# Text rows first in the stacks, first entry's copies on GpSimd, and the second pair's keys begun ahead of slot 0

## The chip, the cores and the metric

The kernel runs on one core of a Trainium2 chip. The metric is the device time of one execution in microseconds. The engines are TensorE (PE, with PEld for its weight loads), VectorE (DVE), ScalarE (ACT), GpSimd (POOL) and SyncE (SP, which here only issues DMAs). In the profile a time stands from the start of the span; `L747` is line 747 of the kernel before. The PE clock is given as a share of full speed.

## The reference, cut to what matters

Two cross-attention layers follow each other over 16 batch entries of 256 rows, with 20 heads of 16. The 256 context rows are split into text and image rows: 77 and 179 in the first layer, 252 and 4 in the second. The first layer, which the change touches, computes

```python
q_h, k_h, v_h = heads(x @ Wq), heads(text @ Wk), heads(text @ Wv)
text_out = softmax(q_h k_h * scale) v_h
text_probs = softmax((q . k_text) * scale)          # over all channels, one for all heads
sem = (text_probs @ text) . ip * scale
fused = q_h ip_k_h * scale + 0.5 * sem               # ip = image rows, their own Wk_ip, Wv_ip
out = (text_out + softmax(fused) * mask @ ip_v_h) @ Wout + bout + x
```

and the second has the same parts with normalized semantic scores. All data is fp32. A product is made from a high part (rounded to fp32r) and a low part (what the rounding left), in three matmuls: high by high, high by low, low by high.

## The kernel before

The first layer has 80 slots: slot k is entry b = k // 5 and group g = k % 5 of four heads. The second layer has 80 more. In a slot, `score0(k + 2, t)` (L747) makes plain scores from which VectorE takes row maxima (L748, L749); `maxima0` (L755 to L759) turns the maxima, copies them to tile `mt` and sends them by four small DMAs into the query stack; `turned0(k, t)` (L771) makes the transposed scores less the maxima, ScalarE takes the exponential (L774), GpSimd multiplies by the semantic factor `rs` (L777); `attend0(k - 1)` (L806) multiplies with the values and VectorE and GpSimd settle the result (L817 to L824, into `hsn`).

Scores come from two stacks in rings of four, `qs[k % 4]` and `ks[k % 4]`, 127 rows each: 48 field rows (high, low, high parts of 16 channels), 77 text rows that carry the semantic part, and 2 rows for the maxima (in `ks`: two indicator rows). `stacks0(k, parts)` fills them: "K" and "Q" fetch field rows from DRAM (`kd`, `qd`), "T" fetches the text rows of the query stack from `tph`, "M" those of the key stack from `M`. Text rows are the same for all groups of an entry, so they are fetched only for g < 4. In the kernel before, all four parts are DMAs on SP's queue, and the `tph` and `M` tiles have three extra rows so that one DMA fills rows 48 to 127. `fields()` writes the indicator rows and those extra rows.

Keys are made for pairs of entries. `keys0(c)` loads the context of pair c in four tiles (`context`, `in_turn`: a load, a ScalarE cast for the high part, a subtraction for the low part) and then makes keys in six products, text (`wk0`, tile `wA`) and image (`wki0`, tile `wB`) for each of three row blocks. `queries0(b)` loads an input, splits it (`split`, L284 to L286: cast, subtraction of two tiles, and the low part of rows 64 to 127 of the third tile), and projects it (`project`, L611 and L614). `weights4(0)` loads the output weights (`wF`), which entry 0 needs first in slot 7.

What sets the order: `begin()` is everything ahead of slot 0, and there all engines run in the order in which the code is written. Generators are cut into steps; `parts(x)` makes one step of task x, and what a task has left is made in the slots at the times in its list (`FIRST`, `shifted`; -1 means before slot 0). In the slots only TensorE keeps the written order; that of the others is settled when the program is built. SP's DMAs signal eight semaphores in turn, so each issue waits until the DMA eight before it has landed.

## Time and profile before

| | |
|---|---|
| timed runs | 1486.59 us, median of 3 (1484.38 to 1487.22) |
| profiled execution | 1494.71 us, with a span of 1492.9 us |
| granted PE clock, mean | 0.986 |
| busy share of the span | PE 95%, DVE 79%, ACT 59%, POOL 81% |
| first layer's slots | from the first L771 at 50.6 us on |
| moved by DMA | 234.32 MB, 157 GB/s on average; 220 GB/s in the first 100 us |

A row of the timeline has start, length, engine, line, operation, out<-in, shape and count, and in brackets the idle time before it with what ended it. A row of the windows has the stretch, its length, busy time of each engine with its count of instructions, the granted clock, the mean busy share of the DMA engines and GB/s.

### The profile page before, as it was taken

To read this page: it belongs to the slowest core of one execution; us is meant where nothing else is said; L and a number is where in the kernel's file an instruction comes from. 1 tells how busy PE (TensorE), PEld (TensorE's weight loads), DVE (VectorE), ACT (ScalarE), POOL (GpSimd) and SP (SyncE) were. 2 spreads that over 40 slices of the span, in tenths; PEclk is the share of its full clock that TensorE was granted. 3 is DMA by queue.
4 is the path that set the end of the run, shared out by engine and by line. 5 is a ranking of instruction groups with operands and counts; after the bars stand their busy time and mean duration, and the time that the engine had idled before them with its cause. 6 is when DMAs were issued, how large, how long until landed. Compare 5 with 4: busy or idle time off the path is not lost.

```text
span 1492.9 us, 36116 instructions
## 1 busy us (share of the span) xinstructions
PE 1425.3 (95%) x12740; PEld 1153.4 (77%) x12740; DVE 1176.8 (79%) x2595; ACT 885.7 (59%) x1975; POOL 1213.8 (81%) x1302
## 2 busy tenths in 40 slices
PE   7799999999999999789999999999999999999998
PEld 7677888888888787567777777777777777777766
DVE  5578777777777776878887888888878887888787
ACT  6355565656565555456665666666656665666563
POOL 4369797979797877788698789878987888788887
PEclk9899999999999998999999999999999999999999
DMA  7967777777777775775544444434444444443311
GB/s 235 235 180 200 207 222 206 217 205 222 202 226 204 209 200 148 194 208 151 166 99 132 117 123 120 132 115 125 121 126 121 124 118 124 123 126 102 111 32 54
DMA packets 230986, 234.32 MB, mean 157 GB/s; under 512 B 39127, under 2 KB 200678, under 8 KB 230790
## 3 DMA queue, kind: packets, MB, share of 16 engines
q1 hardware_dynamic: 228598, 230.71, 55.6%
q8 instruction: 102, 1.67, 0.5%
q10 hardware_dynamic: 2208, 1.30, 0.4%
q14 instruction: 78, 0.64, 0.1%
HBM read 118.04 MB, written 77.04 MB: 131 GB/s over the span
## 4 chain that ended last, share of the span: by engine, by line
PE 74%; DVE 8%; DMA 6%; POOL 4%; issue 4%; ACT 3%; SPq 1%; ACTq 0%; DVEq 0%; POOLq 0%
PE X L945 15%; PE X L241 14%; PE P L806 6%; PE X L611 5%; PE P L957 5%; PE S L747 5%; PE P L967 4%; PE T L771 4%; PE T L896 3%; PE S L902 3%; PE X L614 2%; PE X L251 2%; PE X L580 2%; DVE mn L749 1%; POOL P L777 1%
## 5 line engine op out<-in xcount | busy, mean ns | idle before, releaser
L777 POOL TENSOR_TENSOR P<-P,rs 128x512 f32<-128x512 f32 x320 | 414.9, 1319 | 85.1 <-ACT P L774 84.0
L936 POOL TENSOR_TENSOR wt<-P,ctb 128x512 f32<-128x512 f32 x318 | 408.4, 1308 | 74.8 <-ACT ctb L934 74.7
L945 PE MATMUL X<-ctb,gm 128*128 128x512 f32 x1120 | 306.3, 402 | 5.8 <-DVE wt L946 5.7
L774 ACT ACTIVATE P<-T 128x512 f32<-128x512 f32 x320 | 175.5, 594 | 155.7 <-PE T L771 106.7
L946 DVE TENSOR_TENSOR wt<-X,wt 128x512 f32<-128x512 f32 x320 | 216.0, 681 | 42.3 <-PE X L945 37.6
L945 PEld LDWEIGHTS X<-ctb,gm 128*128 128x128 f32 x1120 | 195.0, 188 | 39.3 <-DVE wt L946 8.7
L916 ACT ACTIVATE P<-T 128x512 f32<-128x512 f32 x320 | 173.0, 593 | 75.2 <-PE T L896 72.2
L934 ACT ACTIVATE ctb<-P 128x512 fp32r<-128x512 f32 x320 | 186.5, 627 | 36.8 <-PE X L945 34.2
L904 DVE TENSOR_REDUCE mn<-S 128x4 fp32r<-128x1008 f32 x160 | 191.4, 1197 | 0.0
L749 DVE TENSOR_REDUCE mn<-S 128x4 fp32r<-128x716 f32 x160 | 142.3, 889 | 0.0
L806 PE MATMUL P<-P,vr 128*32 128x256 f32 x1920 | 127.4, 397 | 5.4 <-DVE tmp L823 1.9
L747 PE MATMUL S<-ks,qs 125*128 125x256 f32 x640 | 115.7, 304 | 3.9 <-DVE mn L749 1.9
L747 PEld LDWEIGHTS S<-ks,qs 125*128 125x128 f32 x640 | 87.5, 192 | 38.7 <-issue 20.7
L1036 POOL TENSOR_TENSOR r<-u,rs 128x40 f32<-128x40 f32 (+2 forms) x17 | 108.7, 6394 | 3.0 <-DVE u L1033 2.9
L771 PE MATMUL T<-qs,ks 127*128 127x256 f32 x640 | 107.6, 290 | 1.2 <-DMA qs<-mt 0.9
L817 DVE STREAM_TRANSPOSE nt<-P 128x512 f32<-128x512 f32 x80 | 56.9, 712 | 53.2 <-PE P L806 52.7
L806 PEld LDWEIGHTS P<-P,vr 128*32 128x32 f32 x1920 | 56.9, 112 | 47.6 <-issue 7.6
L771 PEld LDWEIGHTS T<-qs,ks 127*128 127x128 f32 x640 | 90.9, 195 | 3.3 <-DMA qs<-mt 0.7
L748 DVE TENSOR_REDUCE mn<-S 128x4 fp32r<-128x308 f32 x160 | 74.4, 465 | 22.2 <-PE S L747 22.0
L957 PE MATMUL P<-P,v1t 128*32 128x256 f32 x1280 | 85.7, 385 | 0.0
L967 PE MATMUL P<-wt,zone 128*32 128x256 f32 x1280 | 84.4, 379 | 0.0
L241 PE MATMUL X<-wC,cta 128*128 128x324 f32 (+1 forms) x474 | 78.6, 312 | 0.0
(305 smaller groups left out, 2979.9 us busy)
## 6 DMA issues: line engine op xcount, KB each, us to landing
qd<-q SPq DMA_DIRECT2D x96, 256.0 KB
qs<-tph SPq DMA_DIRECT2D x64, 320.0 KB
rawc<-in_cT_dram SPq DMA_DIRECT2D x60, 256.0 KB
qs<-qd SPq DMA_DIRECT2D x80, 192.0 KB
ks<-kd SPq DMA_DIRECT2D x80, 192.0 KB
ks<-kd SPq DMA_DIRECT2D x160, 96.0 KB
qs<-qd SPq DMA_DIRECT2D x160, 96.0 KB
kd<-kst SPq DMA_DIRECT2D x57, 256.0 KB
```

The source lines that it names most:

```text
L241: last = mm(out, lhs(a, k), rhs(b, k), start=i == 0, stop=i == len(terms) - 1)
L747: mm(sp[:, h], Q[: XROW + T0, h, t * 128 : (t + 1) * 128], K[: XROW + T0, h], start=True, stop=True)
L771: mm(st[p][:, j], K[:KS0, 2 * p + j, t * 128 : (t + 1) * 128], Q[:KS0, 2 * p + j], start=True, stop=True)
L774: exp = anchor(nc.scalar.activation(pt, st[p], AF.Exp, scale=SCALE))
L777: anchor(nc.gpsimd.tensor_mul(pt, pt, rs[:, t : t + 1].to_broadcast([128, 2, S])))
L806: mm(pv[32 * s : 32 * s + 32, o : o + S], v[:, vt, h : h + 32], P[k, s // 2][:, t, s % 2], start=vt < 2, stop=vt != 1,)
L904: anchor(nc.vector.tensor_reduce(maxes[k + 2][:, t], sp[:, :, :T1], axis=AX.X, op=ALU.max))
L916: anchor(nc.scalar.activation(P[k, u][:, t], st[u], AF.Exp, scale=SCALE))
L934: nc.scalar.activation(R[k, u][:, t], P[k, u][:, t], AF.Copy, scale=0.5)
L936: anchor(eng.tensor_sub(W[k, u][:, t], P[k, u][:, t], f(R[k, u][:, t])))
L945: mm(yp, gm[:, gb], R[k, u][:, kt], start=i == 0, stop=i == len(blocks[n]) - 1)
L946: nc.vector.tensor_mul(W[k, u][:, n], yp, W[k, u][:, n])
```

## The change

The stacks are laid out anew: text rows first (0 to 76), then 48 field rows (`FIELD` = 125 is their end), then the two rows of maxima. `tph` and `M` lose their three extra rows, and `fields()` writes four wide indicator DMAs and nothing else. For entry 0 the text rows of all four stacks are copied by GpSimd, for the other entries still by DMA. In `begin()` the loads, casts and subtractions of the second pair's context are made among the steps of the second entry (one subtraction on VectorE, three on GpSimd), and its first key product is cut into four pieces, which stand in slot 0. The third entry's input is loaded and split in `begin()` too. In each `queries0` after the first, the third tile's low part is a GpSimd subtraction of 64 rows in place of a VectorE operation on 128. `mt` has two buffers. The output weights are loaded in slots 4 to 5 in place of 2.6 to 3.2, and the context of entry 2 in the second layer is subtracted by GpSimd.

```diff
-TR = T0 + 3
+FIELD = T0 + 48
...
-        yield from in_turn(parts, wait, "rawc raw" if b == 2 and n == 2 else "rawc", nc.gpsimd if wait and b != 2 else nc.vector, n == 2 and b >= 2)
+        yield from in_turn(parts, wait, "rawc raw" if b == 2 and n == 2 else "rawc", nc.vector if not wait else nc.gpsimd if n == 1 or b != 2 else (nc.vector,) + (nc.gpsimd,) * 3, n == 2 and b >= 2)
...
-        order(nc.vector.scalar_tensor_tensor(hl[:, 2], f(hl[:, 2]), neg, src[:, 2], op0=ALU.mult, op1=ALU.add))
+        if neg is None:
+            order(eng.tensor_sub(hl[64:, 2], src[64:, 2], f(hl[64:, 2])))
+        else:
+            order(nc.vector.scalar_tensor_tensor(hl[:, 2], f(hl[:, 2]), neg, src[:, 2], op0=ALU.mult, op1=ALU.add))
...
         for i in range(SIZES["NR"]):
-            dma(ks[i][XROW + T0 : KS0, :, :T0], ind0r[:2, :T0].unsqueeze(1).to_broadcast([2, 4, T0]))
-        for i in range(2):
-            dma(buf("M", [TR, 2, S], FR, bufs=SIZES["M"])[T0:, 0], ind0r)
-            dma(buf("tph", [TR, 2, S], FR, bufs=2)[T0:, 0], ind0r)
+            dma(ks[i][FIELD:KS0], ind0r.unsqueeze(1).to_broadcast([2, 4, S]))
...
-                prod_m(kp, w, m, lambda s, k: ct(s, k)[:, :, lo:hi], 4)
+                if c == 1 and not m + a:
+                    for k in range(4):
+                        for i, (x, y) in enumerate(((0, 0), (0, 1), (1, 0))):
+                            mm(kp, w(x, k, m), ct(y, k)[:, :, lo:hi], start=k + i == 0, stop=k + i == 5)
+                        if k < 3:
+                            yield
+                else:
+                    prod_m(kp, w, m, lambda s, k: ct(s, k)[:, :, lo:hi], 4)
...
-        xs = split(x, tmask[:, 5:6], nc.gpsimd, "hq") if b else xs0.pop()
+        xs = split(x, None, nc.gpsimd, "hq") if b else xs0.pop()
...
             if part == "K":
-                anchor(dma(K[0:XROW], stack_rows(kd[0][b // 2][:, :, b % 2], g)))
+                anchor(dma(K[T0:FIELD], stack_rows(kd[0][b // 2][:, :, b % 2], g)))
...
+                copy = dma if b else lambda out, in_: nc.gpsimd.tensor_copy(out, f(in_))
                 if part == "T":
-                    dma(Q[XROW : XROW + TR], tph[:, 0:1].to_broadcast([TR, 4, S]))
+                    copy(Q[:T0], tph[:, 0:1].to_broadcast([T0, 4, S]))
...
-        mt = buf("mt", [8, S], FR)
+        mt = buf("mt", [8, S], FR, bufs=2)
...
-    FIRST = {"k0": [-1, 0.6, 0.6, 0.6, 1, 1.2, 1.6, 1.6, 2, 2.2, 2.6], "s0": [-1, -1, -1, -1, -1, 0.2, 0.6]}
+    FIRST = {"k0": [-1, -1, -1, -1, -1, 0.2, 0.2, 0.6, 0.6, 1.2, 1.6, 2, 2.2, 2.6], "s0": [-1, -1, -1, -1, -1, 0.2, 0.6]}
...
-    task(("w4", 0), [2.6, 2.8, 3, 3.2], lambda: weights4(0), ("k0", 1))
+    task(("w4", 0), [4, 4.2, 4.6, 5], lambda: weights4(0), ("k0", 1))
...
+        for k in range(SIZES["NR"]):
+            stacks0(k, "M")
...
-        stacks0(0, "TQK")
+        for k in range(SIZES["NR"]):
+            stacks0(k, "T")
+        stacks0(1, "Q")
+        stacks0(2, "Q")
         get(*s0)
         parts(q1, q1)
-        stacks0(1, "M")
+        for k in range(3):
+            stacks0(k, "K")
         parts(v0)
-        stacks0(1, "TQK")
         parts(v0)
         get(*v0)
+        parts(q2)
+        parts(k1)
+        stacks0(3, "QK")
```

Three places show how instructions move. The first is TensorE around slot 0, where the second pair's first key product stands (`wA` holds the text key weights, `cta` and `ctb` the pair's context). Before:

```order
L747 MATMUL S<-ks_101,qs_97 128x256 x4
L771 MATMUL T<-qs_95,ks_99 128x256 x4
L747 MATMUL S<-ks_101,qs_97 128x256 x4
L771 MATMUL T<-qs_95,ks_99 128x256 x4
L755 MATMUL X<-ident_r,mn_576 8x128 x2
L747 MATMUL S<-ks_102,qs_98 128x256 x4
L771 MATMUL T<-qs_96,ks_100 128x256 x4
L241 MATMUL X<-cta_81,wA_85 128x156 x3
L241 MATMUL X<-cta_82,wA_85 128x156 x3
L241 MATMUL X<-ctb_83,wA_85 128x156 x3
L241 MATMUL X<-ctb_84,wA_85 128x156 x3
```

And of the change (its L755, L779 and L763 are L747, L771 and L755 of before):

```order
L755 MATMUL S<-ks_101,qs_97 128x256 x4
L779 MATMUL T<-qs_95,ks_99 128x256 x4
L383 MATMUL X<-cta_81,wA_85 128x156 x3
L383 MATMUL X<-cta_82,wA_85 128x156 x3
L755 MATMUL S<-ks_101,qs_97 128x256 x4
L779 MATMUL T<-qs_95,ks_99 128x256 x4
L383 MATMUL X<-ctb_83,wA_85 128x156 x3
L383 MATMUL X<-ctb_84,wA_85 128x156 x3
L763 MATMUL X<-ident_r,mn_585 8x128 x2
L755 MATMUL S<-ks_102,qs_98 128x256 x4
L779 MATMUL T<-qs_96,ks_100 128x256 x4
L241 MATMUL X<-cta_81,wB 128x360 x3
```

The twelve key matmuls move from behind slot 1's first turned scores to two places among slot 0's, and the image key product (`wB`) comes ahead of the first attend. From the third input's projection on, TensorE's order is the same in both.

The second place is GpSimd from the values' low parts (`wD`) to slot 0's multiplication (`P` with `rs`). Before:

```order
L1273 TENSOR_TENSOR wD<-rs_115,wD 128x320
L436 MEMSET M_260 77x2x77
L1273 TENSOR_TENSOR wD<-xc_116,wD 128x320 x2
L436 MEMSET M_261 77x2x77
L777 TENSOR_TENSOR P_120<-P_120,rs_114 128x512
L777 TENSOR_TENSOR P_121<-P_121,rs_114 128x512
```

And of the change:

```order
L1282 TENSOR_TENSOR wD<-xc_116,wD 128x320 x2
L724 CAST qs_95<-tph_439 77x1024
L724 CAST qs_96<-tph_439 77x1024
L724 CAST qs_97<-tph_439 77x1024
L724 CAST qs_98<-tph_439 77x1024
L285 TENSOR_TENSOR hq_230<-xq_91,hq_230 128x512
L287 TENSOR_TENSOR hq_230<-xq_91,hq_230 64x256
L169 TENSOR_TENSOR cta_82<-rawc_118,cta_82 128x512
L169 TENSOR_TENSOR ctb_83<-raw,ctb_83 128x512
L444 MEMSET M_282 77x2x77
L169 TENSOR_TENSOR ctb_84<-raw,ctb_84 128x512
L785 TENSOR_TENSOR P_120<-P_120,rs_114 128x512
```

Four copies into the query stacks, the third entry's split and three context subtractions now stand between the two; four copies into the key stacks (`CAST ks<-M`, 77 by 4 by 179) stand earlier, ahead of the second entry's split.

The third place is SP's queue up to the maxima of slot 0 (`qs_95<-mt`). Before:

```order
L86 DMA qs_97<-tph_263 80x4x256
L86 DMA ks_101<-M_260 80x4x179
L86 DMA ks_102<-kd_70 48x4x256
L86 DMA qs_98<-qd_309 48x1024
L759 DMA qs_95<-mt_222 2x256 x4
L86 DMA qs_98<-tph_263 80x4x256
L86 DMA ks_102<-M_260 80x4x179
L86 DMA rawc_117<-in_cT_dram 128x512
L86 DMA rawc_118<-in_cT_dram 128x512
L86 DMA raw<-in_cT_dram 128x512 x2
L759 DMA qs_96<-mt_222 2x256 x4
L86 DMA qd_495<-q_145 128x2x256 x3
```

And of the change:

```order
L86 DMA xq_91<-in_xT_dram 128x3x256
L86 DMA rawc_117<-in_cT_dram 128x512
L86 DMA rawc_118<-in_cT_dram 128x512
L86 DMA raw<-in_cT_dram 128x512 x2
L86 DMA qs_98<-qd_303 48x1024
L86 DMA ks_102<-kd_70 48x4x256
L86 DMA kd_70<-kst_158 128x2x256
L86 DMA kd_70<-kst_158 128x256
L86 DMA qd_498<-q_144 128x2x256 x3
L86 DMA qd_498<-q_144 64x2x256
L86 DMA qd_498<-q_144 64x256
L767 DMA qs_95<-mt_222 2x256 x4
```

The four context loads (`rawc`, `raw`), the second entry's queries to DRAM and part of its keys now stand ahead of slot 0's maxima; slot 1's maxima follow directly behind.

More of the change, by code (lines that the diff above doesn't have):

```diff
@@ L200, in in_turn @@
             if i:
-                halves(*ahead.pop(0), eng, wait)
+                halves(*ahead.pop(0), eng[i - 1] if isinstance(eng, tuple) else eng, wait)
             for j in new:
@@ L210, in in_turn, with weights @@
                 yield
-    def weights(w_d, tag, half=None, wait=0, raw="raw"):
+    def weights(w_d, tag, half=None, wait=0, raw="raw", later=False):
         n = w_d.shape[1]
@@ L217, in weights @@
         heads = tag != "wF"
-        yield from in_turn([(rows(w_d, k)[:, : n if heads else CH], *rounded(w[:, k], heads)) for k in range(kt)], wait, raw)
+        yield from in_turn([(rows(w_d, k)[:, : n if heads else CH], *rounded(w[:, k], heads)) for k in range(kt)], wait, raw, later=later)
         if half is not None:
@@ L443, in tokens0 @@
         yield
[L444 removed]
+        return M
     v1t, gmt = [], []
@@ L518, in weights4 @@
     def weights4(l):
-        wo.append((yield from weights((wo0_d, wo1_d)[l], "wF", tmask[:, 4:5], (0.1, 0.3)[l], "rawc")))
+        wo.append((yield from weights((wo0_d, wo1_d)[l], "wF", tmask[:, 4:5], (0.1, 0.3)[l], "rawc", not l)))
     def weights3():
@@ L1362, in begin @@
         parts(v1)
+        parts(k1)
         get(*v1)
         parts(s1)
+        parts(k1, k1)
         score0(1, 1)
@@ L1367, in begin @@
         maxima0(1, nc.sync)
-        for make in held:
-            make()
-        parts(k0)
+        parts(k1)
+        parts(k0, k0)
         resid0.append(load(xT_d[0], "xc"))
```

51 lines of the change are left out of this document (25 added, 26 removed).

## The prediction

> **What bounds the kernel now.** I read the windows of busy time first, to see in which stretches TensorE is short of work, then its timeline there, then the timelines of the engine that each of its waits names.
>
> ```profile
> span 1492.9 us, 36116 instructions
> ...
> core 0: us, PE busy (x) PEld busy (x) DVE busy (x) ACT busy (x) POOL busy (x), PEclk, DMA share, GB/s
> 0.00:57.00 57.00, 44.80 (x288) 41.66 (x288) 32.68 (x94) 32.91 (x84) 22.87 (x45) 1.00 0.84 230
> 57.00:71.60 14.60, 10.66 (x68) 8.19 (x66) 9.05 (x14) 3.71 (x8) 8.07 (x8) 0.65 0.85 240
> 71.60:83.42 11.82, 10.47 (x90) 9.35 (x90) 7.68 (x16) 6.32 (x16) 7.37 (x10) 1.00 0.77 216
> 83.42:102.74 19.32, 17.64 (x145) 13.99 (x146) 12.38 (x32) 8.49 (x22) 11.49 (x12) 0.91 0.61 167
> ...
> 320.00:380.00 60.00, 59.64 (x568) 51.56 (x566) 45.29 (x110) 36.19 (x87) 53.55 (x53) 1.00 0.79 220
> ```
>
> In a steady stretch of the first layer (320 to 380) TensorE is busy 59.64 of 60 us: there the end is set by TensorE's own work, which this change leaves as it is, matmul for matmul. In the first 102.74 us it is busy 83.57, and from 57 to 71.6 its granted clock is 0.65. A change to the order at the start can win only there, and a microsecond won there goes through to the end, since TensorE is the bound behind it and its order from the third input's projection on is unchanged. Where the time lies, in TensorE's timeline, with the idle time before a row and its releaser in brackets:
>
> ```profile
> 50.63 0.92 PE L771 MATMUL T<-qs,ks 127*128 127x256 f32 x4
> 52.17 0.74 PE L747 MATMUL S<-ks,qs 125*128 125x256 f32 x4 [0.63 <-DVE mn L749]
> 54.29 0.23 PE L755 MATMUL X<-ident_r,mn 128*8 128x128 f32 x1 [0.84 <-DVE mn L749]
> 55.64 0.93 PE L771 MATMUL T<-qs,ks 127*128 127x256 f32 x4 [0.42 <-DMA qs<-mt]
> 59.49 0.72 PE L241 MATMUL X<-cta,wA 128*128 128x156 f32 x2 [2.31 <-DVE cta L169]
> 61.16 1.35 PE L241 MATMUL X<-ctb,wA 128*128 128x156 f32 x5 [0.75 <-DVE ctb L169]
> 62.45 2.79 PE L806 MATMUL P<-P,vr 128*32 128x256 f32 x24
> ...
> 69.09 0.79 PE L241 MATMUL X<-cta,wA 128*128 128x156 f32 x6
> ...
> 71.60 1.10 PE L611 MATMUL X<-hq,wE 128*128 128x256 f32 x7 [0.89 <-POOL hq L285]
> ...
> 76.57 1.50 PE L806 MATMUL P<-P,vr 128*32 128x256 f32 x24
> ...
> 83.42 0.76 PE L241 MATMUL X<-cta 128*77 128x192 f32 x6 [1.35 <-DVE q L169]
> ...
> 92.98 0.23 PE L755 MATMUL X<-ident_r,mn 128*8 128x128 f32 x1 [1.19 <-DVE mn L749]
> ```
>
> The sum is made against the profiled execution, 1494.71 us, which is 1.8 us more than its span and 8.1 us over the runs' median of 1486.59. I carry the difference over to the median unchanged.
>
> **The change part by part.** The second pair's context is the late thing between 56 and 62 us. Its loads stand behind slot 0's maxima on SP's queue, and its subtractions on VectorE between the maxima reductions:
>
> ```profile
> 24.67 3.31 SPq L86 DMA_DIRECT2D qd<-q  x5
> ...
> 44.88 2.62 SPq L759 DMA_DIRECT2D qs<-mt  x4
> ...
> 50.14 1.33 SPq L86 DMA_DIRECT2D rawc<-in_cT_dram  x2
> ...
> 57.66 1.78 DVE L169 TENSOR_TENSOR cta<-rawc,cta 128x512 fp32r<-128x512 f32 x1
> ```
>
> In the change the loads stand directly behind the three key stacks and one input, with 14 DMAs less ahead of them (8 of text rows, 4 of indicator rows into `M` and `tph`, a second load of the indicator, and `hop`). With about 0.65 us an issue (2.62 for 4) they go out from 37 to 40 us, and land by 45. ScalarE casts the tiles among the second entry's steps, the last behind slot 1's maxima at about 49.5. GpSimd's three subtractions (1.3 us each, as L777's below) end at about 51.3 us. TensorE asks for the first two tiles after slot 0's first turned scores, at about 51.1, and for the others after one key half, scores and turned scores (some 1.8 us) at 52.9.
>
> *Up to slot 0's turned scores I count nothing.* TensorE waits 1.33 and 0.45 us for stacks before 45 us, and both should shrink; but the turned scores at 50.63 need the maxima's DMAs, and these now stand behind more bytes.
>
> ```profile
> 34.00:38.00 4.00, 4.00 (x30) 4.00 (x29) 0.00 (x0) 0.97 (x2) 0.00 (x0) 1.00 0.83 211
> ...
> 50.00:55.00 5.00, 3.53 (x23) 2.82 (x22) 2.77 (x5) 3.24 (x8) 2.78 (x3) 1.00 0.92 282
> ```
>
> From 33.4 us SP would queue seven field stacks (192 KB each by their shapes, 1344 KB), an input and four context tiles (384 and 1024 KB), and keys and queries to DRAM (384 and 960 KB). At 211 GB/s for stacks (34 to 38 us) and 282 for the rest (50 to 55 us, the same context loads) that is 6.4 and 9.8 us: done at 49.6, and the maxima behind them land at about 50.5. So the first turned scores start where they start now. What was won ahead of them is slack.
>
> *From there on the waits count.* The 0.63 and 0.84 us at 52.17 and 54.29 are VectorE's maxima, one score bank behind; they stay as latencies, but the twelve key matmuls now stand in them. Six of these take about 0.63 to 0.79 us (69.09), so 1.47 us of wait hold nearly all of that work. The 0.42 us for slot 1's maxima goes: their DMAs no longer stand behind the context loads. The 2.31 and 0.75 us for the context go, 3.06 in all. **Sum so far 4.95.**
>
> *The clock.* From 57 to 71.6 us the mean clock is 0.65, which loses 14.6 x 0.35 = 5.1 us; half of the 3.06 us of waiting lay in it (1.5), so its work lost 3.6. The attend at 62.45 shows it: 2.79 us for what takes 1.50 at 76.57. The drop follows a stretch in which TensorE was poorly filled. With the waits filled it should not come. **8.55.**
>
> *The third input's split* (0.89 us at 71.60) stood on GpSimd behind slot 1's multiplications. It is now done before slot 0. **9.44.** *The wait of 1.35 us at 83.42* is for a query row block that VectorE gives out late:
>
> ```profile
> 81.27 1.43 DVE L169 TENSOR_TENSOR wF<-rawc,wF 128x256 fp32r<-128x256 f32 x1
> ...
> 82.96 0.41 DVE L169 TENSOR_TENSOR q<-X,q 128x256 fp32r<-128x256 f32 x1
> ```
>
> The output weights' subtraction just ahead of it moves two slots on, so this goes too. **10.8 us in sum.** The 1.19 us at 92.98 and the clock of 0.91 behind it also follow a `wF` subtraction, but the weights may do the same in their new place: between 0 and 3.4 us (1.19, two waits of 0.24, and 9% of 19.32), of which I take none.
>
> *What is added lies on GpSimd.* The copies and the half-height subtraction don't occur in the trace of before, so I bound them:
>
> ```profile
> 49.30 0.23 POOL L436 MEMSET M<- 77x154 f32 x1 [15.82 <-PE X L699]
> ...
> L386 POOL CAST kb<-kst 128x308 fp32r<-128x308 f32 x14 | 6.2, 441 | 4.3 <-DVE kst L169 3.5 <-DVE rn L461 0.8
> ...
> L824 POOL TENSOR_TENSOR hsn<-tmp 128x128 f32<-128x128 f32 x80 | 40.9, 511 | 5.2 <-DVE tmp L823 5.1
> ...
> L1273 POOL TENSOR_TENSOR wD<-rs,wD 128x320 fp32r<-128x320 f32 x2 | 1.7, 876 | 0.3 <-DMA qd<-q 0.3
> ...
> L777 POOL TENSOR_TENSOR P<-P,rs 128x512 f32<-128x512 f32 x320 | 414.9, 1319 | 85.1 <-ACT P L774 84.0
> ```
>
> A copy has one input, as the cast of 308 elements in 441 ns: 1.43 ns an element, with a start in it. By length alone 1024 and 716 elements take 1.47 and 1.03 us; at the price of a two-input row (1319 ns for 512) 2.6 and 1.8. Nothing excludes less than the first. I take 1.0 and 0.8, the cast's row being nearest and its start not growing: 7.2 us for eight, up to 17.8. The subtraction of 256 elements lies between 511 (128) and 876 ns (320): 0.75 us. With the two splits' parts (1.5), a moved split (1.3) and three context subtractions (1.3 each) GpSimd gets about 14 us of new work between 24 and 52 us. It was idle 15.82 us in one piece there, and 2.7 more before slot 0's multiplication. So these cost nothing; without that cover slot 0's multiplication would start later by what is over.
>
> In the slots the subtraction comes 13 times, 9.8 us of GpSimd, and VectorE is rid of this:
>
> ```profile
> L286 DVE SCALAR_TENSOR_TENSOR hq<-hq,tmask,xq 128x256 fp32r<-128x256 f32 x14 | 11.7, 835 | 1.6 <-ACT hq L284 1.5
> ...
> POOL P L777 <- ACT P L774: 58.0, 56, 4.3
> ```
>
> GpSimd waits 58 us for ScalarE between 140 and 640 us, so it has room; TensorE waits for VectorE's maxima there now and then. I take zero, between a loss of 9.8 and a gain of 9.
>
> The Trainium skill, GPSIMD Engine Reference, section Performance versus the Vector engine, speaks against this part: it has VectorE about twice as fast at elementwise work. By that and VectorE's 486 ns median the subtraction would be some 0.97 us, and the slots' load 12.6 us; the sum is the same while it stays covered. No row of before shows it at this size.
>
> **The rivals.** *DMA bandwidth is the new bound* (0.17). If the bytes ahead of slot 0's maxima all move at 211 GB/s, they end at 52.8 rather than 49.6 us, and TensorE stands 3 us at its first turned scores. For it: the four key stacks were late before. Against it: the 2.2 MB of text rows and their issues are gone. It leaves 10.8 - 3.2 = 7.6 at best, and 4 if the clock falls once more, halfway **1480.8**.
>
> *The half clock stays* (0.04), since it doesn't come from these waits.
>
> ```profile
> 54.00:56.00 2.00, 1.29 (x8) 0.96 (x8) 1.43 (x2) 1.98 (x4) 2.00 (x3) 1.00 0.57 209
> 56.00:58.00 2.00, 1.18 (x7) 0.85 (x6) 2.00 (x4) 1.85 (x5) 2.00 (x2) 0.75 0.98 326
> ```
>
> The clock fell inside 56 to 58, after four microseconds in which TensorE was busy 2.47. No long idle stretch precedes it. If something else set it, 3.6 us stay: 7.2 won, **1479.4**. The Trainium skill, TensorE: Matmul & The Clock Gate, Part 1, has the clock halved after at least one idle window of some 3.4 us, and by that rule these short waits would not be the cause. The trace disagrees: it fell without such a window.
>
> *More than the sum* (0.10): the weights' stall at 92.98 goes as well and VectorE's relief shortens some waits for maxima, 3.4 + 2: **1470.4**.
>
> *GpSimd becomes late* (0.05): copies at the two-input price, 10.6 us more than taken. Slot 0's multiplication would end near 62 rather than 57 us, the waits stay open, and the clock falls: about 2 us won, **1484.6**.
>
> *Slower* (0.06): the new subtraction stands ahead of GpSimd's `hsn` addition in the slots, VectorE's transposition waits for that in order, and the maxima stand behind the transposition. If each of 13 entries costs TensorE 0.75 us and a brief half clock like that after 92.98 (0.09 x 19.32 / 1.19 = 1.5 us for each us of wait, so 1.1 for 0.75), 24 us go and 10.8 come: **1499.8**. It decides from (10.8 + 3) / 13 = 1.06 us an entry. Against it: GpSimd's 58 us of waiting.
>
> *The gain is lost at the turn of the layers* (0.03), where the built order of VectorE and ScalarE shifts: within 0.2%.
>
> **How the numbers follow.** The forecast, a gain of 8 to 14 us, has 0.55: 1486.6 - 10.8 = **1475.8**. The range reaches over the half clock and DMA rivals and most of the greater gain, **1468 to 1484**; outside lie the slow rival, GpSimd's lateness, the loss at the turn and a little on the low side. Faster by over 0.2% (3 us, about what a measurement of this kernel can tell from none) are the forecast, DMA, clock and the greater gain: 0.86. Within 0.2%: 0.08. Slower: 0.06.
>
> **What would show it.** Right: the turned scores of slot 0 start near 50.6 us, TensorE's row of the third input's projection starts near 61 rather than 71.6, the clock is 1.00 from 50 to 70 us, and the steady stretch reads as before. Wrong: a wait for `qs<-mt` of over 2 us ahead of the first turned scores; a `CAST qs<-tph` above 1.5 us; TensorE waiting for `cta` or `ctb` again; or more waits for maxima between 100 and 600 us, which would put the loss on GpSimd's subtraction.

## The result and the profile after

The changed kernel takes 1530.98 us (median of 6 runs, 1524.03 to 1545.66) against 1486.9 us before (6 runs, 1484.38 to 1493.43): 1.0292 of the time, 95% interval 1.0245 to 1.0339. It is slower by some 44 us, where a gain of 10.8 was forecast. The profiled execution took 1524.89 us, with a span of 1523.1.

The windows of busy time of the changed kernel, read as before:

```profile
50.00:57.00 7.00, 6.50 (x38) 6.10 (x38) 2.88 (x6) 2.86 (x6) 6.25 (x6) 0.76 0.38 105
57.00:71.60 14.60, 14.60 (x138) 12.70 (x137) 8.80 (x20) 7.12 (x16) 9.92 (x11) 1.00 0.69 222
83.42:102.74 19.32, 19.32 (x188) 16.62 (x181) 14.42 (x34) 12.62 (x31) 17.70 (x19) 1.00 0.67 193
320.00:380.00 60.00, 55.09 (x525) 47.59 (x525) 44.76 (x98) 31.94 (x76) 46.96 (x45) 0.97 0.63 177
```

From 57 to 71.6 us the start did what was forecast: the clock is 1.00 and TensorE is busy throughout. But a half clock has not gone altogether. It came earlier and for a shorter time: the mean clock is 0.76 from 50 to 57 us, which loses 7 x 0.24 = 1.7 us, where 5.1 were lost from 57 to 71.6 before. And the steady stretch, where TensorE was busy 59.64 of 60 us, now has it busy 55.09. Its timeline, at the places of the forecast and at the first large wait:

```profile
51.49 0.80 PE L383 MATMUL X<-cta,wA 128*128 128x156 f32 x6
58.48 1.50 PE L814 MATMUL P<-P,vr 128*32 128x256 f32 x24
62.27 1.15 PE L619 MATMUL X<-hq,wE 128*128 128x256 f32 x8
72.65 0.71 PE L241 MATMUL X<-cta 128*77 128x192 f32 x6
113.28 1.22 PE L755 MATMUL S<-ks,qs 125*128 125x256 f32 x4 [4.96 <-DVE mn L757]
```

The token scores of `cta` start at 72.65 us, at 83.42 before: 10.8 us won. From 113 us on it goes the other way. Since TensorE's order from there on is the same, the first matmul of one slot's attend can be compared between any two runs. This table, worked out from the traces, has its start before, and in the other runs the distance from that, in us (spare, gap and pin are experiments told below; the pin is the narrow one):

```
slot  before   after  tile back  tile alone  spare   gap   gap+pin  before again
   4   105.02  -13.6      -15.3        -2.4    0.4  -12.6    -12.7          -0.8
  16   197.54   -6.6      -11.0         4.9    8.2   -9.9     -8.5          -3.5
  40   378.32   14.7      -11.3        23.6   38.0    2.0     -5.0          -0.1
  60   533.40   26.7      -11.4        36.1   56.3   13.8      0.6          -0.0
 150  1398.53   30.2       -5.8        37.2   57.1   16.2      4.3          -0.6
```

From 13.6 us ahead the change falls to 30.2 us behind: 43.8 us are lost, nearly all up to slot 61 and hardly any in the second layer. At slot 8 every run of the table gains some 2.7 us, since the first profile of before lost them there to a hold of its own, told below. The losses come in steps: 6.4, 6.5, 5.5, 5.5, 5.5 and 4.4 us in slots 7, 17, 27, 37, 47 and 57 (the even places, as I call them), and 1.9 to 2.6 us in slots 11, 21, 31, 41, 51 and 61 (the odd places), some with 0.7 to 1.25 more a slot later. Who is waited for, between 100 and 640 us (total, times, longest), first after, then before:

```profile
PE S L755 <- DVE mn L757: 27.1, 7, 5.0
PE X L619 <- ACT mt L765: 6.0, 5, 1.2
PE X L763 <- DVE mn L757: 5.8, 5, 2.3
PE X L619 <- DVE ho L285: 4.3, 6, 1.8
PE X L619 <- DVE ho L289: 3.0, 6, 0.6
```

```profile
PE X L755 <- DVE mn L749: 9.1, 10, 1.8
PE X L611 <- ACT mt L757: 4.0, 5, 0.8
```

The large one is the scores' wait for VectorE's maxima, at the even places. VectorE's timeline at the first of them, and GpSimd's:

```profile
104.86 6.77 DVE L285 TENSOR_TENSOR ho<-hT,ho 128x512 fp32r<-128x512 f32 x1 [1.00 <-ACT ho L284]
111.56 0.47 DVE L289 SCALAR_TENSOR_TENSOR ho<-ho,tmask,hT 128x256 fp32r<-128x256 f32 x1
111.95 0.47 DVE L756 TENSOR_REDUCE mn<-S 128x4 fp32r<-128x308 f32 x1
112.34 0.89 DVE L757 TENSOR_REDUCE mn<-S 128x4 fp32r<-128x716 f32 x1
```

```profile
103.19 2.56 POOL L785 TENSOR_TENSOR P<-P,rs 128x512 f32<-128x512 f32 x2
105.70 1.29 POOL L169 TENSOR_TENSOR cta<-rawc,cta 128x512 fp32r<-128x512 f32 x1
106.94 0.47 POOL L832 TENSOR_TENSOR hsn<-tmp 128x128 f32<-128x128 f32 x1
107.36 1.28 POOL L169 TENSOR_TENSOR cta<-rawc,cta 128x512 fp32r<-128x512 f32 x1
108.59 2.50 POOL L785 TENSOR_TENSOR P<-P,rs 128x512 f32<-128x512 f32 x2
115.70 2.54 POOL L785 TENSOR_TENSOR P<-P,rs 128x512 f32<-128x512 f32 x2 [4.62 <-ACT P L782]
```

VectorE's subtraction for `ho` takes 0.67 us where nothing is in its way. Here it takes 6.77: it ends 0.5 us after GpSimd's unbroken run ends at 111.09. The maxima's reductions stand behind it in VectorE's queue, TensorE's scores wait for them, ScalarE then has no scores to exponentiate, and only that breaks GpSimd's run. I call this a hold. TensorE's wait is 4.96 us here and 4.2 to 4.5 at the other five places, and its clock falls with it:

```profile
110.00:118.00 8.00, 4.72 (x25) 4.72 (x26) 6.83 (x13) 1.77 (x4) 3.38 (x3) 0.57 0.23 70
```

What a step costs beyond its wait (5.5 us for a wait of 4.4 at the usual place) fits this half clock; the two were not separated. The same place before:

```profile
118.35 1.66 DVE L285 TENSOR_TENSOR ho<-hT,ho 128x512 fp32r<-128x512 f32 x1 [1.36 <-ACT ho L284]
```

```profile
118.16 1.30 POOL L169 TENSOR_TENSOR cta<-rawc,cta 128x512 fp32r<-128x512 f32 x1
119.42 0.92 POOL L824 TENSOR_TENSOR hsn<-tmp 128x128 f32<-128x128 f32 x1
120.29 1.46 POOL L169 TENSOR_TENSOR cta<-rawc,cta 128x512 fp32r<-128x512 f32 x1
121.72 5.04 POOL L777 TENSOR_TENSOR P<-P,rs 128x512 f32<-128x512 f32 x4
```

There VectorE got its turn behind the first `cta` subtraction, and GpSimd's `hsn` took 0.92 instead of 0.47 us. GpSimd's run was as unbroken here, and went on to 126.76 us: an unbroken run alone does not make a hold. The Trainium skill, SBUF — State Buffer, section Who interferes with whom, says that a VectorE instruction with two SBUF inputs contends with a GpSimd instruction that reads SBUF, and that the ports that they share are locked by one of them at a time. Both pictures agree that it blocks; 6.77 us behind six instructions is more than one instruction's length.

### The profile page after: what moved, and what is told of

Read it like the earlier page. It is cut to its first block, busy times and chain, and to the rows that moved or that the text cites. A ratio compares the mean times of both kernels' runs of the same rounds, so it can differ in the third digit from the quotient of the medians.

```text
span 1523.1 us, 36028 instructions
## 1 busy us (share of the span) xinstructions
PE 1431.1 (94%) x12740; PEld 1160.2 (76%) x12740; DVE 1191.9 (78%) x2575; ACT 887.1 (58%) x1975; POOL 1229.2 (81%) x1330
## 4 chain that ended last, share of the span: by engine, by line
PE 73%; DVE 9%; POOL 5%; issue 4%; DMA 4%; ACT 3%; ACTq 0%; SPq 0%; POOLq 0%; DVEq 0%
PE X L953 15%; PE X L241 13%; PE P L814 6%; PE X L619 5%; PE S L755 5%; PE P L965 5%; PE P L975 4%; PE T L779 4%; PE T L904 3%; PE S L910 3%; PE X L622 2%; PE X L251 2%; PE X L588 2%; DVE mn L757 2%; POOL P L785 1%
## 5 line engine op out<-in xcount | busy, mean ns | idle before, releaser
L755 PE MATMUL S<-ks,qs 125*128 125x256 f32 x640 | 118.3, 309 | 29.5 <-DVE mn L757 27.7
L755 PEld LDWEIGHTS S<-ks,qs 125*128 125x128 f32 x640 | 89.7, 197 | 63.9 <-DVE mn L757 31.8
L779 PE MATMUL T<-qs,ks 127*128 127x256 f32 x640 | 108.5, 293 | 1.4 <-DMA qs<-mt 1.0
L779 PEld LDWEIGHTS T<-qs,ks 127*128 127x128 f32 x640 | 92.4, 199 | 3.2 <-DMA qs<-mt 1.8
L619 PE MATMUL X<-ho,wF 128*128 128x256 f32 x496 | 79.7, 302 | 15.0 <-ACT mt L765 6.0
L619 PEld LDWEIGHTS X<-ho,wF 128*128 128x128 f32 x496 | 70.2, 204 | 25.2 <-ACT mt L765 7.1
```

Of the source, the lines that this page charges most:

```text
L619: mm(pp, w(s, k, m), a[:, t], start=i == 0, stop=last and i == len(terms) - 1)
L755: mm(sp[:, h], Q[:FIELD, h, t * 128 : (t + 1) * 128], K[:FIELD, h], start=True, stop=True)
L779: mm(st[p][:, j], K[:KS0, 2 * p + j, t * 128 : (t + 1) * 128], Q[:KS0, 2 * p + j], start=True, stop=True)
```

## The experiments

Single times stand beside one run of the kernel before on the same chip; where an interval is given there were more.

### Is it the third tile, and which engine's part of it

Four kernels. The first puts the tile back on VectorE in the slots (the start keeps its changes):

```diff
-        xs = split(x, None, nc.gpsimd, "hq") if b else xs0.pop()
+        xs = split(x, tmask[:, 5:6] if b > 2 else None, nc.gpsimd, "hq") if b else xs0.pop()
```

> The kernel after, but from entry 3 on the low part of the third tile of a layer 0 input is a subtraction on VectorE again, as before; the start keeps all of its changes. Theory (the third tile's subtraction on GpSimd shifts the built order and GpSimd's phase, so that VectorE's subtraction for ho, 128x512 with two SBUF inputs, is held off by GpSimd for about 6 us at one place in each pair of entries): the 6.8 us rows of ho are gone, no wait of L755 for mn over 1 us between 100 and 600 us, and the 13.7 us won by 100 us stay: about 1472 us, 0.990 of before. Rival (what the start moves has shifted the built order in the slots, and the third tile is not to blame): the long ho rows stay, about 1525 us, 1.026 of before.

Measured: 1488.74 us (10 runs, 1483.61 to 1500.7), 1.0001 of before, 0.9972 to 1.0030. Neither time was expected: the loss is gone, but so is the gain. The second adds the tile's move alone to the kernel before:

```diff
+        if neg is None:
+            order(eng.tensor_sub(hl[64:, 2], src[64:, 2], f(hl[64:, 2])))
...
-        xs = split(x, tmask[:, 5:6], nc.gpsimd, "hq") if b else xs0.pop()
+        xs = split(x, None if b > 1 else tmask[:, 5:6], nc.gpsimd, "hq") if b else xs0.pop()
```

> The kernel before, with one part of the change alone: from entry 2 on the low part of the third tile of a layer 0 input is a half-height subtraction on GpSimd. Theory: the loss of the slots comes with this part alone, 6 long ho rows of about 6 us and 6 small stalls of 2 us, so about +43 us: 1522 to 1535 us. Rival (the start's changes shift the order): 1487 us within 4. Second rival (GpSimd's own 13 x 0.73 us): about 1496 us, with ho rows no longer than 1.9 us.

Measured: 1533.02 us, 1.0295 (1.0249 to 1.0341). The move alone brings the whole loss. The third leaves the tile on VectorE and gives GpSimd a subtraction that nobody needs; the fourth gives the tile to neither.

```diff
+        if tag == "hq" and eng is nc.gpsimd and extra:
+            order(eng.tensor_sub(spare[64:], src[64:, 2], f(hl[64:, 2])))
         order(nc.vector.scalar_tensor_tensor(hl[:, 2], f(hl[:, 2]), neg, src[:, 2], op0=ALU.mult, op1=ALU.add))
...
-        xs = split(x, tmask[:, 5:6], nc.gpsimd, "hq") if b else xs0.pop()
+        xs = split(x, tmask[:, 5:6], nc.gpsimd, "hq", extra=b > 1) if b else xs0.pop()
```

> The kernel before, with its VectorE operation for the third tile kept, and from entry 2 on the same half-height subtraction done a second time on GpSimd, into a tile that nobody reads. Theory (0.73 us more on GpSimd just ahead of the odd entries' hsn addition moves GpSimd's later work to where it holds VectorE's ho off): long ho rows of about 6 us at the even places, and 1520 to 1535 us, though VectorE's work is that of before. Rival (VectorE without the third tile, in another built order, is what meets GpSimd): no ho row over 2 us, 1485 to 1500 us.

```diff
-        order(nc.vector.scalar_tensor_tensor(hl[:, 2], f(hl[:, 2]), neg, src[:, 2], op0=ALU.mult, op1=ALU.add))
+        if neg is not None:
+            order(nc.vector.scalar_tensor_tensor(hl[:, 2], f(hl[:, 2]), neg, src[:, 2], op0=ALU.mult, op1=ALU.add))
...
-        xs = split(x, tmask[:, 5:6], nc.gpsimd, "hq") if b else xs0.pop()
+        xs = split(x, None if b > 1 else tmask[:, 5:6], nc.gpsimd, "hq") if b else xs0.pop()
```

> The kernel before, with the low part of the third tile of a layer 0 input left out from entry 2 on (it is computed nowhere; its 64 rows keep the rounded value). Theory (GpSimd's 0.73 us is the trigger): neither engine has the work, no long ho rows, 1480 to 1490 us. Rival (VectorE's relief shifts its order): long ho rows as in the change, about 1525 us.

Measured: 1551.78 us with the useless subtraction (before beside it: 1488.41), 1486.78 with neither. The rows of `ho`'s subtraction between 100 and 640 us (minimum, median, longest in ns), in this order: tile back, tile alone, useless subtraction, left out:

```profile
L285 DVE TENSOR_TENSOR ho<-hT,ho x14: 668/1026/5886, 103.0 to 621.5; 128x512 fp32r<-128x512 f32 x14
```

```profile
L285 DVE TENSOR_TENSOR ho<-hT,ho x13: 673/1451/6296, 116.0 to 627.8; 128x512 fp32r<-128x512 f32 x13
```

```profile
L285 DVE TENSOR_TENSOR ho<-hT,ho x12: 674/3322/6479, 118.7 to 596.8; 128x512 fp32r<-128x512 f32 x12
```

```profile
L285 DVE TENSOR_TENSOR ho<-hT,ho x14: 668/1308/1661, 116.6 to 618.8; 128x512 fp32r<-128x512 f32 x14
```

So GpSimd's added 0.73 us does it, and VectorE's relief is not needed for it: with the relief alone (left out) the time is that of before, and with the useless subtraction and no relief 63 us are lost, more than was expected. These two times are of one run each. With the tile back, one hold is left, at 103 us (5.89 us), which cost 6.8 us there.

### Odd or even entries

```diff
-        xs = split(x, None, nc.gpsimd, "hq") if b else xs0.pop()
+        xs = split(x, tmask[:, 5:6] if b > 2 and b % 2 == 0 else None, nc.gpsimd, "hq") if b else xs0.pop()
```

(and with `b % 2` for the even ones alone.)

> The kernel after, with the third tile's subtraction on GpSimd for odd entries only (from entry 4 on the even ones have it on VectorE). Theory (what counts is GpSimd's lateness at the even places, where cta's subtractions follow two multiplications; only the odd entries' subtraction stands just ahead of that): the long ho rows stay, 1515 to 1530 us. Rival (any of them does it, by its time alone): half of the loss, about 1503 us.

> The kernel after, with the third tile's subtraction on GpSimd for even entries only (from entry 3 on the odd ones have it on VectorE). Theory: no long ho row behind the first place, 1484 to 1492 us. Rival: half of the loss, about 1503 us.

Measured: 1520.71 and 1498.59 us (before: 1486.4). Odd alone has five holds of 6.1 to 6.8 us; even alone has none. That bears out the theory on the holds. But even alone, between the range expected and its rival's 1503 us, still loses 1.9 us and more at each odd place: there is a second part to the loss.

### Take the held operation away, ask later, or open a gap

```diff
-        hh = split(hT, tmask[:, 6:7], nc.vector, "ho")
+        hh = split(hT, tmask[:, 6:7], nc.vector if l else nc.gpsimd, "ho")
```

> The kernel after, but in layer 0 the low part of the first two tiles of ho (L285, two SBUF inputs) is a subtraction on GpSimd, not on VectorE. Theory (VectorE's subtraction is held off by GpSimd and the maxima stand behind it): there is nothing to hold off, the six waits of 5.5 us for mn go, GpSimd gets 16 x 1.3 us more: 1490 to 1500 us. Rival (GpSimd itself is too late, by the third tile's 0.73 us each): more work for GpSimd makes it worse, over 1530 us.

Measured: 1524.31 us, 1.0233 (1.0185 to 1.0282), neither as expected. Another VectorE operation with two SBUF inputs took the place of the one that was moved, and was held for up to 7.5 us:

```profile
L289 DVE SCALAR_TENSOR_TENSOR ho<-ho,tmask,hT x13: 520/1174/7474, 106.0 to 605.6; 128x256 fp32r<-128x256 f32 x13
```

The next delays VectorE's ask, by which I mean the start of the row of `ho`'s subtraction, when all that it waits for is there:

```diff
+        if delay:
+            nc.vector.transpose(spare, f(hl[:, 0:2]).rearrange("p k t -> p (k t)"))
         order(eng.tensor_sub(hl[:, 3:5], src[:, 0:2], f(hl[:, 0:2])))
...
-        hh = split(hT, tmask[:, 6:7], nc.vector, "ho")
+        hh = split(hT, tmask[:, 6:7], nc.vector, "ho", delay=not l)
```

> The kernel after, with 0.7 us of useless work more on VectorE: a transposition 128x512 of ho's high part, just ahead of ho's subtraction in layer 0. Theory (what decides is whether VectorE asks before or after GpSimd starts cta's first subtraction; in the kernel after it asks 0.01 to 0.84 us ahead, in the kernel before 0.19 us behind): five of the six asks move behind that start, their ho rows fall from 6.3 to 1.2-1.7 us, and the kernel gets faster by the added work, 1495 to 1508 us. Rival (VectorE is short of time, or GpSimd holds it wherever it asks): the long rows stay, 1525 to 1540 us.

Measured: 1536.47 us (before: 1486.4). That theory fell: five asks came 0.29 to 0.55 us behind the start of `cta`'s subtraction and were held for 5.4 to 5.7 us all the same; one, 0.81 us behind it, got through in 1.02. The next puts a GpSimd operation without an SBUF input into the run:

```diff
+                if wait == 0.25 and i == 1:
+                    queued(nc.gpsimd.memset(spare, 0.0))
```

> The kernel after, with a useless memset of 128x512 (about 0.47 us, no input) on GpSimd between the two multiplications and cta's first subtraction of each layer 0 pair. Theory (VectorE is kept out by an unbroken run of two-input operations on GpSimd): VectorE gets its turn beside the memset, ho rows of 0.7 to 1.8 us instead of 6.3, and 1490 to 1508 us though GpSimd has more to do. Rival (VectorE's subtraction waits for something other than GpSimd's run): long rows as before or longer, 1525 to 1540 us.

Measured: 1510.54 us (before: 1486.4), 2.5 us above the range expected, but 14 below the change's profiled execution, with more for GpSimd to do than in the change. VectorE and GpSimd at the second even place:

```profile
185.62 0.96 DVE L287 TENSOR_TENSOR ho<-hT,ho 128x512 fp32r<-128x512 f32 x1 [1.36 <-ACT ho L286]
```

```profile
183.47 2.56 POOL L788 TENSOR_TENSOR P<-P,rs 128x512 f32<-128x512 f32 x2
185.96 0.54 POOL L203 MEMSET spare<- 128x512 f32 x1
186.44 1.30 POOL L169 TENSOR_TENSOR cta<-rawc,cta 128x512 fp32r<-128x512 f32 x1
```

VectorE runs beside the memset; no row of that subtraction is over 1.5 us from 100 to 640 us. This shows that the hold needs GpSimd's unbroken run of operations that read SBUF: with one in between that only writes, VectorE's subtraction gets through at all six places. The Trainium skill, SBUF — State Buffer, section Who interferes with whom, has it so too: a GpSimd instruction that only writes SBUF does not contend with it. What is left, 24 us, comes nearly all at and around the odd places (slots 9 to 12, 19 to 22 and so on).

### The odd places

In the built order ScalarE's cast of `ho` had moved behind a key block's two evacuations there; after, then before:

```profile
147.34 0.45 ACT L260 CAST kst<-X 64x358 fp32r<-64x358 f32 x1 [0.47 <-PE X L251]
147.81 0.46 ACT L261 COPY both<-X 64x358 f32<-64x358 f32 x1
148.17 0.83 ACT L284 CAST ho<-hT 128x768 fp32r<-128x768 f32 x1
```

```profile
155.78 0.83 ACT L284 CAST ho<-hT 128x768 fp32r<-128x768 f32 x1 [1.20 <-DMA qs<-mt]
156.52 1.08 ACT L774 ACTIVATE P<-T 128x512 f32<-128x512 f32 x2
157.49 0.44 ACT L260 CAST kst<-X 64x358 fp32r<-64x358 f32 x1
```

Set against the attend of slot 10 (143.32 and 153.14 us), the cast starts 4.9 us behind it instead of 2.6. Every kernel that gives GpSimd more is built with this order where nothing pins it, useless memset and subtraction included; before, tile back and left out are not. Two attempts to pin it, both on the kernel with the gap. The first took every last block of a key or query behind `ho`:

```diff
-        nc.scalar.copy(hi, out[:64])
+        queued(nc.scalar.copy(hi, out[:64]), anchors.get("ho"))
```

> The kernel after, with the useless memset ahead of cta's first subtraction on GpSimd, and with ScalarE's cast of ho kept ahead of the casts of a key half's last block (two evacuations of 64x358), as the built order had it before. Theory (the odd places' loss is ScalarE's order: ho's cast 0.9 us later, and TensorE's output projection waits for it): the waits of L619 for mt, ho fall from 13 us to under 5 between 100 and 640 us, the odd places lose under 1 us, 1488 to 1498 us. Rival (it is GpSimd's lateness, the order only follows): the odd places lose 2 us as before, 1505 to 1515 us.

Measured: 1513.74 us, 1.0168 (1.0129 to 1.0207), and it did not settle the cause: TensorE's waits for `mt` and `ho` fell to 0.5 us, as expected, but the pin had also moved the block before behind `ho`, TensorE now waited for that, and the odd places lost 2.8 us and more.

```profile
PE X L768 <- DVE kst L265: 14.2, 5, 2.8
```

The second pins the one block:

```diff
-        nc.scalar.copy(hi, out[:64])
+        high = nc.scalar.copy(hi, out[:64])
+        if hi.shape[-1] == S - T0:
+            queued(high, anchors.get("ho"))
...
-        order(nc.scalar.copy(hl[:, 0:3], src))
+        high = order(nc.scalar.copy(hl[:, 0:3], src))
+        if tag == "ho":
+            anchors["ho"] = high
```

> The kernel after, with the memset ahead of cta's first subtraction, and with ScalarE's cast of ho kept ahead of the evacuation of the second key half's last block alone (64x358), nothing else pinned. Theory (the odd places' loss is that order of ScalarE): L619's waits for mt and ho fall from 12 to under 5 us between 100 and 640 us without a new wait for kst, each odd place loses under 1 us, 1494 to 1502 us. Rival (GpSimd's lateness itself): 1506 to 1515 us.

Measured: 1491.96 us (10 runs, 1487.0 to 1498.48), 1.0011 of before (0.9982 to 1.0040). In the table above the two profiles are 2.0 and -5.0 us from before at slot 40, 16.2 and 4.3 at slot 150: 12 us. TensorE's waits for `ho`'s subtractions fall from 5.8 us in the kernel with the gap to 1.4; the wait named `mt` stays at 6.2, against what was expected. The steps at slots 11, 21, 31, 41 and 51 are gone; those at slots 9, 19, 29, 39 and 49, which had come with the gap (1.5 to 3.1 us), are still there at 1.6 to 3.9. So the order is part of the loss, and with the gap and the pin the time is that of before again. What the start won is still spent: in the profile 17 us are lost behind slot 4 (from -12.7 to 4.3).

### Is a version faster than both

All three have the tile back on VectorE in the slots. The first adds the gap in every pair; the others have it once,

```diff
+                w1["gap"] = w1.get("gap", 0) + (wait == 0.25 and i == 1)
+                if wait == 0.25 and i == 1 and w1["gap"] == 2:
+                    queued(nc.gpsimd.memset(spare, 0.0))
```

one with the wide pin and one with the narrow.

> The kernel after, with the third tile back on VectorE from entry 3 on and the useless memset on GpSimd ahead of cta's first subtraction. Theory (the run with the tile put back lost 5.9 us at its first place to one long ho row of 5.9 us, and the gap takes it away): no ho row over 2 us ahead of 640 us, 3 to 6 us faster than with the tile alone put back, 1481 to 1486 us, 0.995 to 0.999 of before. Rival (what is won at the start is lost again at the turn of the layers, whatever the slots do): 1486 to 1490 us.

> The kernel after, with the third tile back on VectorE from entry 3 on, one useless memset on GpSimd at the first place in the slots, and ScalarE's order pinned as in the other run. Theory (5.9 us were lost at that place alone): no ho row over 2 us, 1479 to 1485 us, 0.994 to 0.998 of before. Rival (what the start wins goes at the turn of the layers in any case): 1486 to 1490 us, within 0.2% of before.

> The kernel after, with the third tile back on VectorE from entry 3 on, one memset on GpSimd at the first place of the slots, and the same narrow pin. Theory: no ho row over 2 us and no loss at the odd places, 1479 to 1485 us, 0.994 to 0.998 of before. Rival (other holds and the turn of the layers take what the start wins): 1486 to 1492 us.

Measured: 1502.36 us, 1.0105 (1.0069 to 1.0140); 1506.6 us, 1.0131 (1.0090 to 1.0173); 1492.02 us, 1.0010 (0.9984 to 1.0037). All three are slower than forecast; the last lies at the upper end of its rival (1486 to 1492). The gap in every pair takes the one hold away and brings the odd places' loss with it, as anything added to GpSimd did; the wide pin costs as above, and a hold of 4.07 us came at another place, 119 us. With the narrow pin the holds of `ho` and the steps of the odd places are gone, as its theory said, but one of 3.67 us for `hq` came at 272.7 us, and between slots 60 and 80, at the turn of the layers, it loses 6.3 us. None beats the kernel before. To see how much of the start there was to win, the kernel before was profiled again:

> The kernel before once more, for a second profile of it: the first one ran 8 us longer than the median of its runs. Theory (the half clock from 57 to 71 us and the waits of the start are in every execution): the same waits up to 100 us, within 2 us, so that the 13.7 us that the change wins there are won against the median too. Rival (that profile had a bad start): this one is 5 to 8 us earlier at 100 us, and 5 to 8 us of the 13.7 were never there to win.

Measured: 1493.52 us, with the start's waits as in the first profile (0.8 us earlier at slot 4). So the theory held at 100 us. But both profiled executions of before (1494.71, 1493.52) stand 5 to 6 us over the median of its timed runs (1488.27 of 23 beside the last kernels, 1482.5 to 1500.7), and each has a hold of its own, at different places:

```profile
132.86 3.67 DVE L286 SCALAR_TENSOR_TENSOR hq<-hq,tmask,xq 128x256 fp32r<-128x256 f32 x1
```

```profile
356.43 3.66 DVE L286 SCALAR_TENSOR_TENSOR hq<-hq,tmask,xq 128x256 fp32r<-128x256 f32 x1
```

The first costs about 2.7 us (slot 8 in the table's runs). The second costs 4.3 us (the second profile is 4.3 us ahead at slot 37 and 0.1 at slot 38). Such chance holds may be a part of the spread between runs of the same kernel; that is argued, not shown.

### The hold by itself

Three small programs with GpSimd chains and one VectorE subtraction 128x512 of two SBUF inputs, asked for at many offsets. The core of the second, where `offset` sets how long ScalarE works before it releases VectorE:

```python
mul(pts[0]); mul(pts[1])
nc.gpsimd.tensor_sub(cta[0][:, 1], raw, f(cta[0][:, 0]))
nc.gpsimd.tensor_add(hsn[:, :, 0], tmp[:, 0], tmp[:, 1])
nc.gpsimd.tensor_sub(cta[1][:, 1], raw, f(cta[1][:, 0]))
mul(pts[2]); mul(pts[3])
...
nc.scalar.copy(ho[:, : 3 * S], hT)
nc.vector.tensor_sub(ho[:, 3 * S :], hT[:, : 2 * S], f(ho[:, : 2 * S]))
```

> No attention is computed here: a chain of 8 multiplications 128x512 back to back on GpSimd, and one VectorE operation that starts a set time into it, in 20 rounds (14 with a two-input subtraction 128x512, each about 0.13 us later than the last; two with one SBUF input; two with one input in PSUM and one in SBUF; two with a chain of GpSimd copies of one input). Theory, as the rows of the two traces have it: a two-input subtraction (0.67 us alone) that arrives early in a multiplication gets through at its end (up to 1.9 us), one that arrives late in it (over about 0.7 us in) waits for the end of the whole chain, up to 9 us; with one SBUF input, or one in PSUM, it takes 0.5 to 0.7 us throughout. Rival (turns are given at each boundary): never over 1.3 + 0.7 = 2.0 us. Second rival (a two-input operation always waits for the chain's end): 5 to 10 us in all 14 rounds.

> No attention is computed here: 36 rounds of a GpSimd chain whose operations wait for semaphores as in the kernel, and one VectorE two-input subtraction 128x512 that starts later from round to round. 20 rounds have the chain of the place in the kernel (two multiplications, cta, hsn, cta, two multiplications) and a VectorE operation released by ScalarE; 8 have eight multiplications, 8 the mixed chain with VectorE delayed by its own copies. Theory (the hold depends on the chain and on where in it VectorE asks): rounds of 1 to 2 us and rounds of over 4 us occur, the latter where it asks ahead of the step from a multiplication to cta. Rival (neither chain nor semaphores matter): no round over 2.0 us, as in the first probe.

> No attention is computed here: 40 rounds of the mixed chain of the second probe, with a scalar_tensor_tensor queued behind VectorE's subtraction; loads from DRAM run beside the first rounds, matmuls beside the first two thirds, eight ScalarE copies beside every second round, and in the last 8 rounds cta's input is loaded by DMA. Theory (traffic of other engines on SBUF is what keeps VectorE from its turn): rounds of over 4 us occur where one kind of traffic runs, and none where it has ended. Rival (something else of the kernel's places): no row over 2.0 us in all 40 rounds.

The subtraction's rows in the three, and of one with one input in PSUM:

```profile
L121 DVE TENSOR_TENSOR ho<-hT,hi x16: 681/935/1782, 4.9 to 211.0; 128x512 fp32r<-128x512 f32 x16
L125 DVE TENSOR_TENSOR ho<-px,hi x2: 680/680/680, 182.7 to 194.5; 128x512 fp32r<-128x512 f32 x2
```

```profile
L144 DVE TENSOR_TENSOR ho<-hT,ho x36: 681/1103/1770, 11.4 to 524.1; 128x512 fp32r<-128x512 f32 x36
```

```profile
L152 DVE TENSOR_TENSOR ho<-hT,ho x40: 846/1212/1829, 12.5 to 575.2; 128x512 fp32r<-128x512 f32 x40
```

All three theories missed: in some 90 rounds with two inputs in SBUF VectorE always got its turn at the next boundary, never over 1.83 us, whatever the offset, the chain of the kernel's place, semaphores, DMA, TensorE or ScalarE beside it. With one input in PSUM it took 0.68 us in both rounds, beside GpSimd's multiplications. So what makes a hold last over several boundaries in the kernel is open; it depends on neither the offset nor the traffic alone.

## Why the prediction was wrong

- *Up to slot 0's turned scores nothing; context waits 3.06 us; third input 0.89; wait at 83.42 1.35.* Right. The turned scores started at 49.62 us, but waited three times for the maxima's DMAs (0.53, 0.25 and 0.22 us) and ended where they ended before (51.66 and 51.55). The keys came at 51.49 without a wait, the third input at 62.27 (71.60 before; the prediction says 61, while its own sum up to there, 9.44, gives 62.2), the token scores 10.77 us earlier. The weights' stall at 92.98, taken as zero in a range to 3.4, went too: 13.6 us in all. One wait of 1.11 us, for `kst` at 75.01, is new.
- *The clock: "with the waits filled it should not come", 3.6 us.* Half right. It came once more, with a mean of 0.76 from 50 to 57 us, so the sign "1.00 from 50 to 70 us" was not met. In other runs with the changed start the mean of these 7 us is 1.00 (tile back), 0.51 (gap) and 0.53 (gap and pin), and they are 15.3, 12.6 and 12.7 us ahead at slot 4, against 13.6 here. That the token scores still came 10.8 us earlier, as summed, is in part luck: 1.7 us were lost that the sum did not have, and what made up for them was not found.
- *What is added lies on GpSimd.* The prices were right: 1038 and 798 ns for the copies (1.0 and 0.8 taken), 736 ns for the subtraction (0.75).
- *"In the slots ... I take zero, between a loss of 9.8 and a gain of 9".* **This is the step that failed.** GpSimd's 58 us of waiting were read as room, and the result is a loss of 43.8 us. With 0.73 us more for GpSimd just ahead of a place with an unbroken run, VectorE's subtraction was held to the end of that run instead of for one operation, which cost 5.5 us there with the half clock; and the built order of ScalarE moved at another place. The prediction's own sign for a loss on this subtraction, more waits for maxima between 100 and 600 us, is what came (27.1 us). "Its order from the third input's projection on is unchanged" was true of TensorE, and stood for the engines that it waits for, where it was not. The bound priced GpSimd's own time and VectorE's, and no interaction of the two. The profile had signs of one: `hq`'s mean of 835 ns against a median of 486, mostly from one row of 3.67 us.
- *The slower rival* (0.06) had the right engine, and the maxima's place behind a VectorE operation, but the wrong wait: a late `hsn`, at 24 us. It was `ho`'s subtraction, kept out by GpSimd's run, at 43.8 us with the odd places.
- *"A microsecond won there goes through to the end" and "I carry the difference over to the median unchanged."* Neither held: with the loss taken out in three ways (tile back, gap with the pin, tile back with the pin) the time is before's within the 0.4% of the intervals, though the start is 11 to 15 us earlier in each profile against before's. Where it goes is only partly seen: with the tile back 6.8 us at the first place and 5.1 between slots 60 and 80, at the turn of the layers (6.3 with the tile back and the pin). The rival of a loss there had a chance of 0.03.

## What to carry to other kernels

Idle time of an engine that another can be kept waiting by isn't free room: before moving 0.7 us to it, look for long rows (the longest against the median) of the other engine's two-input operations, and for what is queued behind them. Where such an operation stands ahead of work that the bounding engine waits for, a gap of 0.5 us in the other's run can be worth ten times its length, as at the even places here. And compare the built order on every engine that the bounding one waits for, not on that one alone.

## What was not expected of the hardware

- A VectorE operation of 0.67 us with two SBUF inputs was held for up to 6.77 us (7.47 for the other form), behind six operations of GpSimd, until that run ended. At the same place before it got through behind one (1.66 us), though the run went on, and in the probes it was never held past one. What decides is open.
- Work added to either engine moved the time by far more than its length, both ways: 0.5 us of memset a pair saved 14 us in all between the two profiles, 0.7 us of subtraction an entry cost 63.
- A product 128x512 with a constant, one SBUF input, took VectorE 1.19 and 1.37 us beside GpSimd's multiplications in the first probe, where 0.5 to 0.7 was expected; its time alone was not measured. GpSimd copies of one input hardly held the two-input one (0.78 and 0.79 us).
- TensorE's clock fell to half with no long wait ahead of it: from 48 to 52 us of the changed kernel TensorE was busy 2.69 of 4 us with a clock of 1.00, and from 53 to 55 the clock was 0.50. With the tile back it was busy 3.01 of these 4 us, and the clock stayed at 1.00.
